# Degree counts of a graph network moved beside the normalising of layer 1, uneven transfers split at 112 partitions, and a preparation shared over three engines

## The chip, the cores and the metric

The kernel runs on one core of a Trainium2 chip. The metric is the device time of one launch in microseconds; the number that stands for a kernel is the median of its runs.

A core has a matrix engine (TensorE, PE in the profile), a vector engine (VectorE, DVE), a scalar engine (ScalarE, ACT), a general engine (GpSimd, POOL) and a queue that only issues transfers (SyncE, SP). Each executes its own instructions in order. Transfers are issued from SP's, ScalarE's and GpSimd's queues.

## What is computed

A graph has 6250 nodes with 128 features and 106250 edges, sorted by destination: 50000 random pairs in both directions and a loop at every node. Four layers follow each other; after each, x becomes layernorm(x + layer(x)).

```python
# layer 0: sums of edge attributes, then an MLP with 512 hidden
agg = segment_sum(edge_attr_128, dst, 6250)
y0  = relu(concat([agg, x]) @ W1 + b1) @ W2 + b2
# layer 1 (GIN): neighbours' sum, MLP with 256 hidden, two batchnorms over nodes
h  = (1 + eps) * x + segment_sum(x[src], dst, 6250)
y1 = relu(bn(relu(bn(h @ W1 + b1)) @ W2 + b2) + x)
# layer 2: two convolutions with the neighbours' mean
conv(x) = (segment_sum(x[src], dst) / count(dst)) @ W_l + b + x @ W_r
y2 = conv2(relu(conv1(x)))
# layer 3 (GAT, 3 heads): softmax over each node's edges, weighted sums, projection
alpha = leaky_relu(a_src[src] + a_dst[dst] + a_edge)
y3 = layernorm(x + gat(x, alpha) @ lin_W + lin_b)   # with its own scale and shift
```

Layer 3 also gives each node a loop of its own, whose edge term is the mean of its edges' terms. For that mean, for the mean of layer 2 and for finding a node's first edge, the kernel needs the number of edges up to each node.

## The kernel before, in words

**Tiles.** Nodes are taken as 50 blocks of 125 (`PB`, `NB5`), in 13 chunks (`CHUNKS`) of four blocks, the last of two. Edges are taken as 833 tiles of 128 (`NT`); as rows they stand in 119 partitions of 896 (`RB`, L). Node features exist twice: node-major (`xn`, 125 partitions) and feature-major (`xt`, 128 partitions).

**Preparation** (L84 to L189). The destinations (`dsti`), the destinations shifted by one edge (`prvi`) and the sources (`srci`) are loaded as 119 rows, 118 or 117 of them in one transfer each, on SP's and ScalarE's queues (L100 to L106). VectorE casts them, TensorE transposes them to tiles (`dsta` and `ix["src"]`), a matmul spreads the first row (`bc`), and VectorE makes differences (`relg`, `relb`) and seven tests of the data (`bad`); `fives` and `far` (L177 to L183) belong to one test. Their outcome is `flag` (L189), which every engine reads to branch into the main path (`general`).

**Sums over neighbours** (`neighbours`, L752 on), once in layer 1 and twice in layer 2. Most of a sum is done as a dense product: the count of edges between nodes, as a bf16 matrix in memory, is streamed by SP in pieces (`piece`) and multiplied with the features split in two bf16 halves (`arena`), in L819 (`sums`). For the last nodes the rows of a table in memory are gathered one tile of 128 edges at a time on GpSimd (L774, `row`), 183 tiles in each convolution, and added up by matmuls with a one-hot (L323, `both`), four groups of three tiles at a time, into `by_node`.

**Layer 1.** After the sums (690 to 1072 us), the second part has two stretches. In the first (pool `l1p`, L904 to L922) each of 13 parts of 500 nodes takes a hidden product (`hidden`, L876), a ScalarE activation (L914), a second product (L918), a ScalarE copy (L919) and VectorE statistics (L858) that free the PSUM tile. Beside it run `loops` (scans along the edges, L1207 to L1211) and `counted` (L529 to L560). In the second (pool `l1x`, L924 to L947) the second batchnorm, relu, residual, transposes (`nodes`, `features`), layernorm and `split` are done chunk by chunk, and table1 is stored (L940).

**`counted`.** For each block GpSimd gathers the destinations of 128 edges that surround each node's place (L416, `nd`, 50 gathers on 125 partitions). VectorE compares and sums them: L543 to L545, ten steps of five blocks. From the result (`upto`) come the places of each node's first edge (`start_of`), the reciprocal of its count (`rcnt`), and its last edge (`lasti`, L559).

**Layer 2** (1251 to 2187 us). `last_sums` (L637 to L642) gathers, for each block, the running sum at the node's last edge (`st`, 50 gathers by `lasti` on GpSimd). Table2 is stored from ScalarE's queue (L999). The second convolution stores x3 (L1049) and scatters the destination terms into `edst` (L1046, on GpSimd).

**Layer 3** (2187 to 3575 us). `edst` is loaded as `ed` (L1076; 119 rows), spread along the edges by scans (`along`, L1196 and L1211), and then 208 batches of edges are weighed and summed; their rows come by GpSimd gathers (L1065).

**What sets the order.** The source is written with generators that are pulled at chosen places (`next(degrees)`). A scheduler then orders the instructions of each engine by its own estimate of times, and inserts semaphore waits; tiles from a pool are reused when their readers are done. So an instruction's place in its engine's queue is fixed when the program is built.

Of the kernel before, what the change touches and what calls it, by code (L numbers as in the profile page):

```python
# [8 lines left out]
F32 = mybir.dt.float32  # L9
I32 = mybir.dt.int32  # L10
AF = mybir.ActivationFunctionType
OP = mybir.AluOpType
AX = mybir.AxisListType
# [6 lines left out]
F = 128  # L20
# [18 lines left out]
RT, RB = 7, 119  # L39
# [16 lines left out]
def gnn_kernel(ctx: ExitStack, tc: tile.TileContext, a: dict, out: bass.AP):  # L56
# [27 lines left out]
    with tc.tile_pool(name="ix", bufs=1) as sp, \  # L84
# [12 lines left out]
        def row(x):  # L97
            return x.rearrange("(p t) -> p t", p=1)

        nc.sync.dma_start(dsti[0:RB - 1, :], d[0:full].rearrange("(p t) -> p t", t=L))  # L100
        nc.sync.dma_start(dsti[RB - 1:RB, 0:E - full], row(d[full:E]))
        nc.scalar.dma_start(prvi[1:RB - 1, :], d[L - 1:full - 1].rearrange("(p t) -> p t", t=L))
        nc.scalar.dma_start(prvi[0:1, 1:L], row(d[0:L - 1]))
        nc.scalar.dma_start(prvi[RB - 1:RB, 0:E - full + 1], row(d[full - 1:E]))
        nc.sync.dma_start(srci[0:RB - 1, :], s[0:full].rearrange("(p t) -> p t", t=L))
        nc.sync.dma_start(srci[RB - 1:RB, 0:E - full], row(s[full:E]))  # L106
        dstf = sp.tile([RB, L], F32, name="dstf")
        nc.vector.tensor_copy(dstf, dsti)
        srcf = sp.tile([RB, L], F32, name="srcf")
        nc.vector.tensor_copy(srcf, srci)  # L110
        for k in range(RT):
            nc.gpsimd.tensor_copy(ix["df"][:, k:k + 1], dstf[:, k * 128:k * 128 + 1])

# [6 lines left out]
        nc.vector.tensor_reduce(bad[:RB, 0:1], vi, AX.X, OP.max)  # L120

        dsta = sp.tile([128, NT], F32, name="dsta")
        for x, to in ((dstf, dsta), (srcf, ix["src"])):
            by_row = to.rearrange("p (r k) -> p k r", k=RT)
            for k0 in range(0, RT, 4):
                kn = min(4, RT - k0)
                p = pp.tile([128, 4, 128], F32, name="xa_p")
                for k in range(k0, k0 + kn):
                    nc.tensor.transpose(p[:, k - k0, :RB], x[:, k * 128:(k + 1) * 128], ident[:RB, :RB])
                nc.vector.tensor_copy(by_row[:, k0:k0 + kn, :], p[:, :kn, :RB])  # L130

        sel = sp.tile([128, 128], F32, name="sel")
        nc.vector.memset(sel, 0.0)
# [2 lines left out]
        for c in range(0, NT, 417):  # L136
            w = min(417, NT - c)
            p = pp.tile([128, 512], F32, name="bc_p")
            nc.tensor.matmul(p[:, :w], lhsT=sel, rhs=dsta[:, c:c + w], start=True, stop=True)
            nc.vector.tensor_copy(bc[:, c:c + w], p[:, :w])  # L140
        relg, relb = ix["relg"], ix["relb"]
        by_g = dsta[:, 0:NG * GT].rearrange("p (g j) -> p g j", j=GT)
        bcg = bc[:, 0:NG * GT].rearrange("p (g j) -> p g j", j=GT)
# [31 lines left out]
        nc.vector.tensor_scalar(bad[:, 6:7], bcg[:, 4 * Q0, 0:1], float(ND), None, op0=OP.is_ge)  # L175

        fives = sp.tile([128, NT], F32, name="fives")  # L177
        nc.vector.tensor_scalar(fives, dsta, -(GD // 2), 1.0 / GD, op0=OP.add, op1=OP.mult)
        nc.vector.tensor_scalar(fives, fives, ROUND, None, op0=OP.add)
        nc.vector.tensor_scalar(fives, fives, -ROUND, None, op0=OP.add)  # L180
        far = sp.tile([128, NT], F32, name="far")
        nc.vector.tensor_tensor(far[:, 0:830], fives[:, 1:831], fives[:, 0:830], op=OP.subtract)
        nc.vector.tensor_reduce(top[:, 0:1], far[:, 0:830], AX.X, OP.min)  # L183
        nc.vector.tensor_scalar(bad[:, 3:4], top[:, 0:1], 1.0, None, op0=OP.is_lt)
        p = pp.tile([128, 512], F32, name="bc_p")
# [1 line left out]
        nbad = sp.tile([1, 1], F32, name="nbad")  # L187
        nc.vector.tensor_reduce(nbad, p[0:1, 0:7], AX.X, OP.add)
        nc.vector.tensor_scalar(flag, nbad, 0.0, None, op0=OP.is_equal)  # L189

    ordered = nc.values_load(flag[0:1, 0:1], min_val=0, max_val=1, skip_runtime_bounds_check_because=FLAG)
    with tc.If(ordered) as cond:
# [10 lines left out]
def by_windows(ctx: ExitStack, tc: tile.TileContext, a: dict, out: bass.AP, consts, ix):  # L203
# [52 lines left out]

    def by_block(table, blocks):
        return table[blocks[0] * PB:(blocks[-1] + 1) * PB, :].rearrange("(b p) f -> p b f", p=PB)

    def over(x, n):  # L260

        return x.rearrange("p (b f) -> p b f", f=1).to_broadcast([PB, x.shape[1], n])
# [266 lines left out]
    def counted(pool):  # L529


        thn = pool.tile([128, NB5], F32, name="node_col")
        nc.gpsimd.iota(thn, pattern=[[PB, NB5]], base=1, channel_multiplier=1,
                       allow_small_or_imprecise_dtypes=True)
        nc.vector.memset(upto[:, 0:1], 0.0)
        nd = pool.tile([128, NB5, 128], I32, name="nd")
        edges_from(a["dst"], n0i[:PB], nd[:PB])
        for c in range(NB5 // M):
            yield
            cs = slice(c * M, (c + 1) * M)  # L540
            up = upto[:PB, 1 + cs.start:1 + cs.stop]
            lt = pool.tile([128, M, 128], F32, name="ndlt")
            nc.vector.tensor_tensor(lt[:PB], nd[:PB, cs], over(thn[:PB, cs], 128), op=OP.is_lt)  # L543
            nc.vector.tensor_reduce(up, lt[:PB], AX.X, OP.add)
            nc.vector.tensor_add(up, up, n0[:PB, cs])  # L545

        shift = pool.tile([PB, 2, PB], F32, name="shifts")
        nxt = pool.tile([128, 2], F32, name="nexts")
        for i, by in enumerate((1.0, float(1 - PB))):
            nc.vector.tensor_scalar(nxt[:, i:i + 1], part, by, None, op0=OP.add)  # L550
            nc.vector.tensor_scalar(shift[:, i, :], iota[:PB, :PB], nxt[:PB, i:i + 1], None, op0=OP.is_equal)
        p = (yield).tile([128, 4, F], F32, name="node_p")[:, 0, :]
        start = p[:PB, 0:NB5]
        nc.tensor.matmul(start, lhsT=shift[:, 0, :], rhs=upto[:PB, 1:], start=True, stop=False)
        nc.tensor.matmul(start, lhsT=shift[:, 1, :], rhs=upto[:PB, 0:NB5], start=False, stop=True)
        nc.vector.tensor_copy(start_of[:PB], start)
        nc.vector.tensor_tensor(rcnt[:PB], upto[:PB, 1:], start, op=OP.subtract)
        nc.vector.reciprocal(rcnt[:PB], rcnt[:PB])
        nc.vector.tensor_scalar(lasti[:PB], upto[:PB, 1:], -1.0, None, op0=OP.add)  # L559
        yield  # L560
# [149 lines left out]
    with tc.tile_pool(name="l0w", bufs=2) as work, \  # L710
# [5 lines left out]
        for blocks in CHUNKS:  # L716
            b0, nb = blocks[0], len(blocks)
            w = nb * PB
            cs = slice(b0 * PB, b0 * PB + w)
            xk = work.tile([128, 4, F], F32, name="xk")  # L720
            xk = xk[:PB, :nb, :]
            nc.sync.dma_start(xk, by_block(a["x"], blocks))
            xc = work.tile([128, 4 * PB], F32, name="xc")
            features(xc[:, :w], xk, tp)
            ht = work.tile([128, 4, 4 * PB], F32, name="ht")
            for m in range(4):
                hp = hps.tile([128, 4 * PB], F32, name="hp")
                ms = slice(m * 128, (m + 1) * 128)
                nc.tensor.matmul(hp[:, :w], lhsT=w1[:, 0, ms], rhs=acc0[:, cs], start=True, stop=False)
                nc.tensor.matmul(hp[:, :w], lhsT=w1[:, 1, ms], rhs=xc[:, :w], start=False, stop=True)  # L730
                nc.scalar.activation(ht[:, m, :w], hp[:, :w], AF.Relu, bias=b1[:, m:m + 1])
            if last is not None:
                last()
            yp = yps.tile([128, 4, F], F32, name="yp")
            for j in range(nb):
                for m in range(4):
                    nc.tensor.matmul(yp[:PB, j, :], lhsT=ht[:, m, j * PB:(j + 1) * PB], rhs=w2[:, m, :],  # L737
                                     start=(m == 0), stop=(m == 3))
            y = work.tile([128, 4, F], F32, name="y")
            y = y[:PB, :nb, :]  # L740
            nc.vector.tensor_tensor(y, yp[:PB, :nb, :], row_over(b2[:PB], nb), op=OP.add)
            nc.vector.tensor_add(y, y, xk)
            layernorm(xn[:PB, b0:b0 + nb, :], y)
            nc.sync.dma_start(by_block(tables[0], blocks), xn[:PB, b0:b0 + nb, :])
            split(xn[:PB, b0:b0 + nb, :], blocks, work)

            def last(b0=b0, nb=nb, cs=cs):
                features(xt[:, cs], xn[:PB, b0:b0 + nb, :], tp)
# [93 lines left out]
    with tc.tile_pool(name="l1", bufs=1) as wp:  # L842
# [81 lines left out]
        with tc.tile_pool(name="l1x", bufs=2) as work, tc.tile_pool(name="zps", bufs=3, space=bass.MemoryType.PSUM) as zps, \  # L924
                tc.tile_pool(name="tps", bufs=2, space=bass.MemoryType.PSUM) as tp:
            last = None
            for blocks in CHUNKS:
# [6 lines left out]
                z = nodes(h0[:, cs], nb, zps)  # L934
                if last is not None:
                    last()
                if b0 < 40:
                    next(degrees)
                layernorm(xn[:PB, b0:b0 + nb, :], z)
                nc.sync.dma_start(by_block(tables[1], blocks), xn[:PB, b0:b0 + nb, :])  # L940
                split(xn[:PB, b0:b0 + nb, :], blocks, work)

                def last(b0=b0, nb=nb, cs=cs):
# [7 lines left out]
    with tc.tile_pool(name="l2", bufs=1) as wp, tc.tile_pool(name="l2w", bufs=2) as work, \  # L951
# [22 lines left out]
        def take(k, p):  # L974
# [3 lines left out]
            def late():  # L978
# [11 lines left out]
                for j in range(0, len(blocks), 2):  # L990
# [5 lines left out]
                                             start=(m_ == 0), stop=(m_ == 1))  # L996
                    nc.scalar.copy(pn[:PB, b0 + j:b0 + j + 2, :], yp[:PB, :, 0, :])
                    nc.vector.tensor_tensor(x[:, j:j + 2, :], x[:, j:j + 2, :], yp[:PB, :, 1, :], op=OP.add)
                nc.scalar.dma_start(by_block(tables[2], blocks), pn[:PB, b0:b0 + len(blocks), :])  # L999
            return late  # L1000

        ends = last_sums()
# [5 lines left out]
    with tc.tile_pool(name="l2bw", bufs=2) as work, \  # L1008
# [8 lines left out]
        def then(k):  # L1017
# [27 lines left out]
            for j in range(nb):  # L1045
                nc.gpsimd.indirect_dma_start(  # L1046
                    out=edst, out_offset=bass.IndirectOffsetOnAxis(ap=start_of[:PB, b0 + j:b0 + j + 1], axis=0),
                    in_=ad[:PB, j, :], in_offset=None)
            nc.scalar.dma_start(by_block(x3, blocks), xw[:PB, :nb, :])  # L1049

        neighbours(None, take, then, tables[2], len(matrix) - 2)
    outer.close()
# [20 lines left out]
    with tc.tile_pool(name="fill", bufs=1) as fp, \  # L1073
            tc.tile_pool(name="fps", bufs=2, space=bass.MemoryType.PSUM) as pp:
        ed = fp.tile([RB, L, 4], F32, name="ed")
        nc.sync.dma_start(ed.rearrange("p t f -> p (t f)"), edst.rearrange("(p t) f -> p (t f)", t=L))  # L1076
        filled = fp.tile([RB, L, H], F32, name="filled")
        along(tc, consts, ix["first"], [ed[:, :, h] for h in range(H)], [filled[:, :, h] for h in range(H)], fp, pp)()
        nc.vector.tensor_add(filled, filled, aeb)
# [796 lines left out]
```

## Time and profile before

| what | value |
|---|---|
| time, median of three runs | 3329.91 us (3328.71 to 3332.3) |
| time of the profiled execution | 3577.21 us |
| its span in the trace | 3575.3 us |
| mean granted clock of TensorE | 0.82 |
| busy: PE, DVE, POOL, ACT | 2624.6, 1837.7, 1671.1, 910.8 us |
| flag ready | 36.3 us |
| sums of layer 1 end | 1072 us |
| layer 1's first stretch, second stretch | to 1173, to 1239 us |
| first sums of layer 2 | 1251 us |
| `ed` loaded | 2207.9 to 2225.4 us |

The profiled execution is 7.4% longer than the median of the others; its durations are read as shares of its own span. In the profile a group line gives the line in the code, the engine, the operation, the written and read tiles with shapes, the number of instructions, then their busy time in us and the mean of one in ns, then the idle time of that engine just before them and what ended it. A timeline line begins with its start and its length in us; the bracket holds the idle time before it and what ended that. A step of the chain is start, length, what.

### The profile page before, as it was taken

To read this page: it belongs to the slowest core of one execution; us is meant where nothing else is said; L and a number is where in the kernel's file an instruction comes from. 1 tells how busy PE (TensorE), PEld (TensorE's weight loads), DVE (VectorE), ACT (ScalarE), POOL (GpSimd) and SP (SyncE) were. 2 spreads that over 40 slices of the span, in tenths; PEclk is the share of its full clock that TensorE was granted. 3 is DMA by queue.
4 is the path that set the end of the run, shared out by engine and by line. 5 is a ranking of instruction groups with operands and counts; after the bars stand their busy time and mean duration, and the time that the engine had idled before them with its cause. 6 is when DMAs were issued, how large, how long until landed. Compare 5 with 4: busy or idle time off the path is not lost.

```text
span 3575.3 us, 43560 instructions
## 1 busy us (share of the span) xinstructions
PE 2624.6 (73%) x14544; PEld 1618.5 (45%) x14544; DVE 1837.7 (51%) x6113; ACT 910.8 (25%) x1657; POOL 1671.1 (47%) x1684
## 2 busy tenths in 40 slices
PE   2788879899995599999787893666565666666565
PEld 1334335544442344445343342555554555555554
DVE  4899994478214800000211122666565666666666
ACT  0587874300002400002100010222222222222222
POOL 3000002277607755430556424666666666666662
PEclk9677779999997599999898896777777777777777
DMA  5588871387751356563665553222222222222221
GB/s 155 167 278 279 274 248 48 105 245 228 220 164 51 82 181 205 182 183 96 184 179 153 169 166 90 52 58 58 54 61 58 56 57 58 55 60 59 57 58 33
DMA packets 333524, 461.85 MB, mean 129 GB/s; under 512 B 43998, under 2 KB 217854, under 8 KB 332933
## 3 DMA queue, kind: packets, MB, share of 16 engines
q1 hardware_dynamic: 250754, 278.98, 26.2%
q0 software_dynamic: 54912, 105.86, 12.4%
q10 hardware_dynamic: 27624, 74.14, 5.6%
q8 instruction: 117, 1.92, 0.2%
q14 instruction: 117, 0.96, 0.1%
HBM read 375.30 MB, written 83.36 MB: 128 GB/s over the span
## 4 chain that ended last, share of the span: by engine, by line
PE 52%; DVE 22%; issue 12%; DMA 4%; POOL 3%; another core or an unknown queue 3%; ACT 2%; DVEq 1%; SPq 0%; ACTq 0%; POOLq 0%
PE sums L819 25%; PE o L1162 10%; DVE okey L616 5%; DVE olow L614 4%; PE w_p L1141 4%; POOL nd L416 2%; DVE w L1151 2%; PE both L323 2%; DVE w L1136 1%; PE yp L995 1%; ACT w L1153 1%; PE yp L737 1%; PE fp L1102 1%; DVE mx L1144 1%
## 5 line engine op out<-in xcount | busy, mean ns | idle before, releaser
L1065 POOL DMA_INDIRECT rows<-x,srca x831 | 841.5, 1013 | 490.3 <-issue 213.4
L819 PE MATMUL sums<-piece,arena 125*128 125x500 bf16 x4500 | 1021.1, 383 | 51.1 <-issue 40.0
L819 PEld LDWEIGHTS <-arena 125*128 125x128 bf16 x4500 | 435.6, 98 | 591.4 <-issue 122.4
L774 POOL DMA_INDIRECT row<-table,srca x549 | 542.1, 987 | 335.7 <-issue 142.5
L1162 PE MATMUL o<-rows,w 128*120 128x132 f32 x2078 | 440.1, 364 | 245.1 <-issue 132.2
L1162 PEld LDWEIGHTS o<-rows,w 128*120 128x120 f32 x2078 | 378.1, 255 | 290.1 <-issue 159.7
L619 ACT CAST arena<-made 128x1000 bf16<-128x1000 f32 (+1 forms) x260 | 313.5, 1262 | 63.9 <-PE made L617 55.9
L1153 ACT ACTIVATE w<-w 128x720 f32<-128x720 f32 x208 | 167.0, 803 | 521.6 <-DVE w L1151 368.5
L617 PE MATMUL made<-okey,olow 128*128 128x250 bf16 x1000 | 248.4, 330 | 62.4 <-ACT arena L619 28.4
L616 DVE TENSOR_SCALAR okey<-iok,key 128x250 bf16<-128x250 bf16 x1000 | 289.6, 290 | 0.0
L1141 PE MATMUL w_p<-ident,w 128*120 128x128 f32 x1248 | 230.7, 328 | 65.1 <-DVE w L1136 39.1
L1144 DVE TENSOR_REDUCE mx<-w_p 120x1 f32<-120x768 f32 x208 | 198.0, 952 | 151.7 <-PE o L1162 82.6
L1151 DVE TENSOR_TENSOR w<-w,both 128x720 f32<-128x720 f32 x208 | 187.1, 900 | 162.0 <-remote 89.1
L614 DVE TENSOR_SCALAR olow<-iob,low 128x128 bf16<-128x128 bf16 x1000 | 254.7, 255 | 0.0
L1141 PEld LDWEIGHTS w_p<-ident,w 128*120 128x120 f32 x1248 | 187.2, 169 | 80.3 <-issue 49.6
L325 ACT COPY by_node<-both 128x128 f32<-128x128 f32 (+1 forms) x48 | 12.7, 265 | 756.6 <-PE both L323 479.8
L334 DVE TENSOR_TENSOR onehot<-iota,relg 128x384 f32<-128x384 f32 x118 | 64.2, 547 | 272.7 <-PE both L323 140.9
L617 PEld LDWEIGHTS <-olow 128*128 128x128 bf16 x1000 | 108.0, 113 | 184.9 <-DVE okey L616 89.6
L1136 DVE TENSOR_TENSOR w<-oh,z 128x720 f32<-128x720 f32 x208 | 186.7, 898 | 0.2 <-DVE acc L1169 0.2
L690 POOL MEMSET ea<- 128x128 f32 x1 | 0.5, 465 | 397.9 <-PE sums L323 397.9
L1168 PE MATMUL both<-ident,on 120*128 120x120 f32 x208 | 70.3, 338 | 108.2 <-DVE w L1151 95.2
L1148 PE MATMUL both<-ident,mx 120*128 120x120 f32 x208 | 73.0, 351 | 91.2 <-DVE acc L1169 69.6
(283 smaller groups left out, 3188.5 us busy)
## 6 DMA issues: line engine op xcount, KB each, us to landing
piece<-edges SPq DMA_DIRECT2D x300, 625.0 KB
edges<-arena ACTq DMA_DIRECT2D x100, 625.0 KB
ea<-in_edge_attr_dram SPq DMA_DIRECT2D x69, 768.0 KB
loop<-x SPq DMA_DIRECT2D x208, 68.0 KB
rows<-x,srca POOLq DMA_INDIRECT x831
row<-table,srca POOLq DMA_INDIRECT x549
eat<-in_edge_attr_dram POOLq DMA_DIRECT2D x28, 236.0 KB
table<-xn SPq DMA_DIRECT2D x24, 250.0 KB
```

Of the source, the lines that this page charges most:

```text
L614: nc.vector.tensor_scalar(o, iob, low[:, g:g + 1], None, op0=OP.is_equal)
L616: nc.vector.tensor_scalar(w, iok, key[:, g:g + 1], None, op0=OP.is_equal)
L617: nc.tensor.matmul(p[:, i, 0:NB5 * GD], lhsT=o, rhs=w, start=True, stop=True)
L619: nc.scalar.copy(to, p[:, 0:n, 0:NB5 * GD].rearrange("p i (h d) -> p i h d", d=GD))
L774: nc.gpsimd.indirect_dma_start(out=r[:, j, :], out_offset=None, in_=table, in_offset=bass.IndirectOffsetOnAxis(ap=ix["src"][:, t:t + 1], a ...
L819: nc.tensor.matmul(p, lhsT=xp[:PB, h, i, :], rhs=t[:PB, :, (h - h0) * SC:(h - h0 + 1) * SC], start=(h == 0 and i == 0), stop=(h == NB5 - 1 ...
L1065: nc.gpsimd.indirect_dma_start(out=r[:, j, :], out_offset=None, in_=x3, in_offset=bass.IndirectOffsetOnAxis(ap=ix["src"][:, BT * b + j:BT ...
L1136: nc.vector.tensor_tensor(w, oh.to_broadcast([128, S, H, BW]), z.rearrange("p j (h w) -> p j h w", w=1).to_broadcast([128, S, H, BW]), op= ...
L1141: nc.tensor.transpose(tp[:, j // 3, j % 3 * 128:(j % 3 + 1) * 128], w[:, j, :, :].rearrange("p h w -> p (h w)"), ident)
L1144: nc.vector.tensor_reduce(mx, tp[:, :, 0:384], AX.XY, OP.max)
L1151: nc.vector.tensor_tensor(wf, wf, mb.rearrange("p (j h) w -> p j (h w)", j=1) .to_broadcast([128, S, H * BW]), op=OP.subtract)
L1162: nc.tensor.matmul(o, lhsT=wf[:, j, :], rhs=rr, start=(j == 0), stop=(j == S - 1))
```

## The change

There are three edits.

**1. The comparisons of `counted`.** They are taken per chunk (twelve times four blocks, once two) instead of ten times five blocks, and are pulled in the second stretch, each before its chunk's layernorm; their scratch tile is `rest` of that stretch's pool. In the built program the comparison of the first chunk stands on VectorE in the first stretch, behind the scans, and the other twelve in the second; `start_of`, `rcnt` and `lasti` come at the end of the second stretch. GpSimd's queue then reads: 5 gathers of `st`, 24 of `row`, 26 of `st`, 12 of `row`, 19 of `st`, 147 of `row`; before it read 50 of `st` and 183 of `row`.

```diff
     def counted(pool):
...
-        for c in range(NB5 // M):
-            yield
-            cs = slice(c * M, (c + 1) * M)
+        for blocks in CHUNKS:
+            work = yield
+            cs, nb = slice(blocks[0], blocks[-1] + 1), len(blocks)
             up = upto[:PB, 1 + cs.start:1 + cs.stop]
-            lt = pool.tile([128, M, 128], F32, name="ndlt")
-            nc.vector.tensor_tensor(lt[:PB], nd[:PB, cs], over(thn[:PB, cs], 128), op=OP.is_lt)
-            nc.vector.tensor_reduce(up, lt[:PB], AX.X, OP.add)
+            lt = work.tile([128, 4, F], F32, name="rest")
+            nc.vector.tensor_tensor(lt[:PB, :nb], nd[:PB, cs], over(thn[:PB, cs], 128), op=OP.is_lt)
+            nc.vector.tensor_reduce(up, lt[:PB, :nb], AX.X, OP.add)
             nc.vector.tensor_add(up, up, n0[:PB, cs])
...
-                if b0 < 40:
-                    next(degrees)
+                degrees.send(work)
                 layernorm(xn[:PB, b0:b0 + nb, :], z)
```

**2. Transfers in two parts.** The loads of `dsti`, `prvi` and `srci` become 112 partitions and the rest (6, 5, 6). A helper stores 112 and 13 partitions in place of 125, for tables 0 and 1 (SP's queue), table2 and x3 (ScalarE's): 52 stores more. `ed` is loaded as 112 partitions on SP's queue and 7 on ScalarE's.

```diff
+    def keep_nodes(queue, table, blocks, x):
+
+        to = by_block(table, blocks)
+        for p0, p1 in ((0, 112), (112, PB)):
+            queue.dma_start(to[p0:p1], x[p0:p1, :len(blocks), :])
...
-        nc.sync.dma_start(dsti[0:RB - 1, :], d[0:full].rearrange("(p t) -> p t", t=L))
+        for p0, p1 in ((0, 112), (112, RB - 1)):
+            nc.sync.dma_start(dsti[p0:p1, :], d[p0 * L:p1 * L].rearrange("(p t) -> p t", t=L))
...
-            nc.scalar.dma_start(by_block(x3, blocks), xw[:PB, :nb, :])
+            keep_nodes(nc.scalar, x3, blocks, xw)
...
-        nc.sync.dma_start(ed.rearrange("p t f -> p (t f)"), edst.rearrange("(p t) f -> p (t f)", t=L))
+        for p0, p1, queue in ((0, 112, nc.sync), (112, RB, nc.scalar)):
+            queue.dma_start(ed[p0:p1].rearrange("p t f -> p (t f)"),
+                            edst[p0 * L:p1 * L, :].rearrange("(p t) f -> p (t f)", t=L))
```

In the built program the last of the four last scatters into `edst` stands two row gathers earlier in GpSimd's queue than before.

**3. Preparation.** The copies of `dsta` and `bc` out of PSUM are ScalarE's, `fives` and `far` are GpSimd's, and the cast, transposes and copies of the sources (still VectorE's) stand last in the source.

```diff
-        srcf = sp.tile([RB, L], F32, name="srcf")
-        nc.vector.tensor_copy(srcf, srci)
...
-        for x, to in ((dstf, dsta), (srcf, ix["src"])):
+
+        def tiles_of(x, to, copy):
...
-                nc.vector.tensor_copy(by_row[:, k0:k0 + kn, :], p[:, :kn, :RB])
+                copy(by_row[:, k0:k0 + kn, :], p[:, :kn, :RB])
+
+        tiles_of(dstf, dsta, nc.scalar.copy)
...
-            nc.vector.tensor_copy(bc[:, c:c + w], p[:, :w])
+            nc.scalar.copy(bc[:, c:c + w], p[:, :w])
...
-        nc.vector.tensor_scalar(fives, dsta, -(GD // 2), 1.0 / GD, op0=OP.add, op1=OP.mult)
-        nc.vector.tensor_scalar(fives, fives, ROUND, None, op0=OP.add)
-        nc.vector.tensor_scalar(fives, fives, -ROUND, None, op0=OP.add)
+        nc.gpsimd.tensor_scalar(fives, dsta, -(GD // 2), 1.0 / GD, op0=OP.add, op1=OP.mult)
+        nc.gpsimd.tensor_scalar(fives, fives, ROUND, None, op0=OP.add)
+        nc.gpsimd.tensor_scalar(fives, fives, -ROUND, None, op0=OP.add)
...
-        nc.vector.tensor_tensor(far[:, 0:830], fives[:, 1:831], fives[:, 0:830], op=OP.subtract)
+        nc.gpsimd.tensor_tensor(far[:, 0:830], fives[:, 1:831], fives[:, 0:830], op=OP.subtract)
...
+        srcf = sp.tile([RB, L], F32, name="srcf")
+        nc.vector.tensor_copy(srcf, srci)
+        tiles_of(srcf, ix["src"], nc.vector.tensor_copy)
```

More of the change, by code (lines that the diff above doesn't have):

```diff
@@ L98, in row @@
             return x.rearrange("(p t) -> p t", p=1)
-        nc.sync.dma_start(dsti[0:RB - 1, :], d[0:full].rearrange("(p t) -> p t", t=L))
+        for p0, p1 in ((0, 112), (112, RB - 1)):
+            nc.sync.dma_start(dsti[p0:p1, :], d[p0 * L:p1 * L].rearrange("(p t) -> p t", t=L))
         nc.sync.dma_start(dsti[RB - 1:RB, 0:E - full], row(d[full:E]))
-        nc.scalar.dma_start(prvi[1:RB - 1, :], d[L - 1:full - 1].rearrange("(p t) -> p t", t=L))
+        for p0, p1 in ((1, 113), (113, RB - 1)):
+            nc.scalar.dma_start(prvi[p0:p1, :], d[p0 * L - 1:p1 * L - 1].rearrange("(p t) -> p t", t=L))
         nc.scalar.dma_start(prvi[0:1, 1:L], row(d[0:L - 1]))
         nc.scalar.dma_start(prvi[RB - 1:RB, 0:E - full + 1], row(d[full - 1:E]))
-        nc.sync.dma_start(srci[0:RB - 1, :], s[0:full].rearrange("(p t) -> p t", t=L))
+        for p0, p1 in ((0, 112), (112, RB - 1)):
+            nc.sync.dma_start(srci[p0:p1, :], s[p0 * L:p1 * L].rearrange("(p t) -> p t", t=L))
         nc.sync.dma_start(srci[RB - 1:RB, 0:E - full], row(s[full:E]))
@@ L743, in by_windows @@
             layernorm(xn[:PB, b0:b0 + nb, :], y)
-            nc.sync.dma_start(by_block(tables[0], blocks), xn[:PB, b0:b0 + nb, :])
+            keep_nodes(nc.sync, tables[0], blocks, xn[:, b0:b0 + nb, :])
             split(xn[:PB, b0:b0 + nb, :], blocks, work)
@@ L936, in by_windows @@
                     last()
-                if b0 < 40:
-                    next(degrees)
+                degrees.send(work)
                 layernorm(xn[:PB, b0:b0 + nb, :], z)
-                nc.sync.dma_start(by_block(tables[1], blocks), xn[:PB, b0:b0 + nb, :])
+                keep_nodes(nc.sync, tables[1], blocks, xn[:, b0:b0 + nb, :])
                 split(xn[:PB, b0:b0 + nb, :], blocks, work)
@@ L998, in late @@
                     nc.vector.tensor_tensor(x[:, j:j + 2, :], x[:, j:j + 2, :], yp[:PB, :, 1, :], op=OP.add)
-                nc.scalar.dma_start(by_block(tables[2], blocks), pn[:PB, b0:b0 + len(blocks), :])
+                keep_nodes(nc.scalar, tables[2], blocks, pn[:, b0:b0 + len(blocks), :])
             return late
```

## The prediction, made before the changed kernel ran

> **What bounds the kernel now.** I read the chain of waits first, to learn which stages end on which engine; then the busy time of each engine in the two stretches that the comparisons leave and enter; then the groups of instructions there; then single lines of the timeline at the start, and where layers 2 and 3 begin.
>
> The chain by engine is mostly TensorE and VectorE, and it names four transfers that the diff touches. Columns of the last two lines: start in us, length in us, what.
>
> ```profile
> PE 52%; DVE 22%; issue 12%; DMA 4%; POOL 3%; another core or an unknown queue 3%; ACT 2%; DVEq 1%; SPq 0%; ACTq 0%; POOLq 0%
> ...
> 3.06 19.52 DMA srci<-in_src_dram
> ...
> 2207.91 17.48 DMA ed<-edst
> ```
>
> The second part of layer 1 has two stretches: hidden layers (about 1084 to 1173 us), then normalising (1176 to 1235). The windows give busy us of each engine (and instruction counts):
>
> ```profile
> core 0: us, PE busy (x) PEld busy (x) DVE busy (x) ACT busy (x) POOL busy (x), PEclk, DMA share, GB/s
> 1084.00:1172.80 88.80, 49.32 (x100) 21.29 (x100) 30.96 (x63) 25.69 (x39) 66.71 (x54) 0.77 0.18 47
> 1176.50:1235.00 58.50, 29.58 (x97) 19.30 (x97) 57.00 (x202) 29.15 (x58) 48.44 (x34) 0.53 0.26 50
> ```
>
> In the first no compute engine is full; in the second VectorE is busy 57.0 of 58.5 us. The groups of the first stretch say what sets its pace:
>
> ```profile
> L416 POOL DMA_INDIRECT nd<-in_dst_dram,n0i x43 | 54.4, 1265 | 13.1 <-issue 13.1
> ...
> L876 PE MATMUL hp<-xn,l1w 128*128 128x500 f32 x42 | 23.3, 664 | 25.6 <-DVE cin L1209 25.6
> ...
> L544 DVE TENSOR_REDUCE upto<-ndlt 125x5 f32<-125x640 f32 x10 | 8.1, 811 | 0.1
> L543 DVE TENSOR_TENSOR ndlt<-nd,node_col 125x640 f32<-125x640 int32 x9 | 7.4, 825 | 47.0 <-DMA nd<-in_dst_dram,n0i 47.0
> ```
>
> VectorE stands idle 47.0 us for nd: a comparison needs five more gathers, GpSimd issues one every 1.265 + 0.30 = about 1.5 us, and behind the waiting comparison stand the statistics (L858) that free TensorE's PSUM. That is the stretch's bound: 50 x 1.5 = 75 us of gathers for 44 us of matmuls.
>
> [...] from 15 to 23 us, with only srci loading, the DMA share is 0.11, two of 16. [...]
>
> **The change part by part.** The sums are made against the profiled execution (3577.2 us, span 3575.3); it is 7.4% longer than the median, 3329.9, and I carry differences over unscaled.
>
> *A, preparation.* The flag (L189) ends at 36.3 and everything waits for it.
>
> ```profile
> 14.54 0.63 DVE L108 CAST dstf<-dsti 119x896 f32<-119x896 int32 x1 [11.24 <-DMA dsti<-in_dst_dram]
> ...
> 26.02 1.01 DVE L144 TENSOR_TENSOR relg<-dsta,bc 128x831 f32<-128x831 f32 x1
> ...
> 36.20 0.14 DVE L189 TENSOR_SCALAR flag<-nbad 1x1 int32<-1x1 f32 x1
> ```
>
> dsti [...] lands at about 7.0 (prvi[...] moves at 276 GB/s or more, dsti and srci at 55): 7.5 gained. From the cast to relg are 11.5 us now, with srci's wait and cast, its copies and a third of fives on VectorE in between; with the four copies on ScalarE I count 7.2 (cast 0.6, transposes 1.3, copies of 0.6 to 1.0 each, table load 1.3 beside the load): 4.3 gained. From relg to the flag are 10.3: fives' two rest steps and far (0.58 + 0.60 + 1.02) leave, srcf's cast and copies (0.6 + 1.5) come; 9.7. fives and far on GpSimd, after its copies and memsets (1.82, 0.27, 2.78): [...] needed at about 14. [...] Sum -7.5 - 4.3 - 0.6 + 1.0 = -11.4 (-8 to -13.5).
>
> *B1, comparisons leave the first stretch.* What remains is TensorE: 13 chunks of 8 passes at 0.42 us = 3.36, 43.7 from 1084, so it ends near 1127.5 instead of 1172.9: -45.4 (-35 to -49). One comparison stays there in the built program, after the scans (L1211, three of about 2.05 us): its gathers have landed.
>
> *B2, they enter the second.* VectorE is full there, so all counts: a compare and a reduce of 125x512 at 0.60 net each (they read 0.82 at 640, ends overlapping; the residual L360 of 512 reads 0.68) and the add 0.09: 1.29 x 11 + 0.75 = +15 (12 to 18). Behind each on VectorE wait the layernorm and the transposes fed by it. Gathers are no wait: chunk c needs gather 4c+3, landed at 1080 + 6c, run at 1132 + 6.2c.
>
> *B3, lasti comes at the end of the second stretch.* Now it is ready at 1157.7 and all 50 gathers of st run under the second stretch:
>
> ```profile
> 1158.00 1.20 POOL L639 DMA_INDIRECT st<-esum,lasti  x1 [1.93 <-DVE lasti L559]
> ...
> 1245.11 1.18 POOL L774 DMA_INDIRECT row<-table,srca  x1 [3.52 <-DMA piece<-edges]
> ...
> 1347.86 0.86 PE L323 MATMUL both<-row,onehot 128*32 128x128 f32 x24
> ```
>
> Built, GpSimd's queue reads st x5, row x24, st x26, row x12, st x19, then rows. With E the end of the last normalising (1238.7 now): st at 1.5 us and rows at 1.25 put the first rows at E+9.0 instead of E+6.4 (+2.8 to TensorE's start), the 24th at E+39, st to E+78, twelve rows to E+93 (2.2 to land: E+95.4, needed at E+91.9), st to E+122, twelve rows to E+137, landed E+138.9. TensorE needs those at 1347.86 = E+109.1. So it loses 29.8 in all (20 to 43: it gets there sooner if the 14 us that it idles on "issue" before 1284 are the profiler's). Then rows take 15 us per group of 20 to 24 on TensorE: GpSimd catches up, one stall. B together: -45.4 + 15 + 29.8 = -0.6.
>
> *C, table stores.* Table2's last store ends on five engines, and the next gather waits 8.35 us behind it and the pieces ("1710.61 L774 row, from piece<-edges"). [...] -3.5 (-1 to -4). Tables 0 and 1: a piece ends last or st is in front: 0. 52 stores more, at 0.3 us of issue: SP's 39 rows lie in queues that wait for data; ScalarE's 26, 8 us over 480 us in which it is a quarter busy at most, hide under sums (L819). If not, +8.
>
> *D, edst and ed.* The last scatter moves past two gathers (2 x 1.25 = -2.5) and its predecessor lands in 2.6 rather than 4.6 beside a shorter x3 store (-1.5; 0 to -2). ed, 17.48 us [...], moves in about 9 [...], the remaining 7 partitions on ScalarE's queue beside it: -8.5 (-4 to -11). VectorE's first scan of layer 3 waits for it 38.66 us: all counts. D: -12.5.
>
> Sum: -11.4 - 0.6 - 3.5 - 12.5 = -28; 3577.2 becomes 3549, and 3329.9 becomes 3302.
>
> **Rivals.**
> - *R1, the gathers' order costs nothing*: TensorE has other work at the third and fourth group, or the gathers are cheaper without the profiler. For: it does idle before them now. Against: q3's rows stand behind 50 st in one queue. Then -28 - 30 = 3272.
> - *R2, slower: the first stretch doesn't shorten.* Its 25.6 us of TensorE idle are put to the scans' carry (cin, L1209), which may keep TensorE's queue on VectorE after the comparisons are gone. B2 and B3 stay. With B1 at nothing: 3302 + 45 = 3347. It decides from a B1 under 17 us, that is a stretch of over 72 us (5.5 a chunk). Against: the chunks at its end, free of nd, run at 3 us each.
> - *R3, a worse stall*: 43 for 30, 3315.
> - *R4, the change doesn't do what it says*: rows of 112 move no faster as something else bounds them; A keeps 7.5, C 3.5, ed 8.5 and 1.5 go: 3302 + 21 = 3323. Against: the 0.11.
>
> **How the numbers follow.** Forecast 0.60 (3285 to 3312), R1 0.11, R2 0.09, R3 0.13, R4 0.07. The range 3278 to 3324 leaves out most of R1 and R2. A measurement of this kernel tells about 0.2%, 6.7 us, from no change: faster is under 3323, which the forecast, R1, R3 and half of R4 give, 0.86; the other half of R4 is no change, with R2's near end 0.06; slower 0.08.
>
> **What would show it.** The flag near 25; the first stretch at 44 to 55 us with no VectorE wait for nd; the second at 73, VectorE full; GpSimd's first st after it; TensorE waiting some 30 us for row before its fourth group of `both`; ed in 9. Wrong it would be if TensorE's carry wait stays, if GpSimd's four operations end after 14 us, or if no stall shows in layer 2.

## The result and the profile after

The changed kernel takes 3317.0 us (median of 7 runs, 3311.7 to 3321.8), the kernel before 3333.2 beside it; the ratio is 0.9946, interval 0.9934 to 0.9958. That is 16 us less, against 28 forecast.

The profiled execution of the changed kernel took 3321.8 us (span 3320.0). The first profile of the kernel before, at 3577 us, holds waits of TensorE that its runs near 3330 us don't have, so differences below are taken from a second profile of before (span 3329.1, run e1) unless the first is named, and ratios from runs side by side.

The two stretches of layer 1's second part in the changed kernel, busy us of each engine, in the same view as in the prediction:

```profile
core 0: us, PE busy (x) PEld busy (x) DVE busy (x) ACT busy (x) POOL busy (x), PEclk, DMA share, GB/s
1067.00:1110.00 43.00, 41.75 (x103) 18.77 (x102) 18.23 (x44) 26.25 (x40) 34.51 (x28) 1.00 0.24 71
1113.00:1186.00 73.00, 30.11 (x98) 19.90 (x98) 72.62 (x241) 31.29 (x61) 20.53 (x16) 0.50 0.21 55
```

The first is now TensorE's, 41.75 of 43.0 us busy, at a granted clock of 1.00 for 0.77; the second is VectorE's as before, and longer. The groups of the first stretch show that nothing waits for `nd` any more. The matmul of `hp` has lost its idle time, and a pass takes 0.58 where it took 0.66 to 0.70 us:

```profile
L429 POOL DMA_INDIRECT nd<-in_dst_dram,n0i x28 | 35.7, 1274 | 8.5 <-issue 8.5
L931 PE MATMUL hp<-h,l1w 128*128 128x500 f32 x48 | 23.5, 588 | 0.3 <-ACT h L927 0.2
L889 PE MATMUL hp<-xn,l1w 128*128 128x500 f32 x45 | 21.6, 582 | 0.0
...
L556 DVE TENSOR_TENSOR rest<-nd,node_col 125x512 f32<-125x512 int32 x1 | 0.7, 693 | 0.1
```

The preparation on VectorE's timeline (start, length, what, and in brackets the idle time before it), from the cast of the destinations to the flag:

```profile
5.94 0.63 DVE L111 CAST dstf<-dsti 119x896 f32<-119x896 int32 x1 [2.63 <-DMA dsti<-in_dst_dram]
...
10.05 1.09 DVE L116 TENSOR_TENSOR firstb<-dstf,prvi 119x896 f32<-119x896 f32 x1 [3.02 <-DMA prvi<-in_dst_dram]
11.18 1.65 DVE L120 SCALAR_TENSOR_TENSOR vi<-firstb 119x896 f32<-119x896 f32 x1
...
13.87 1.01 DVE L148 TENSOR_TENSOR relg<-dsta,bc 128x831 f32<-128x831 f32 x1
...
18.39 1.47 DVE L163 CAST basei<-late 1x61 int32<-1x61 f32 x1
...
22.44 1.02 DVE L187 TENSOR_REDUCE top<-far 128x1 f32<-128x830 f32 x1
...
25.33 0.15 DVE L193 TENSOR_SCALAR flag<-nbad 1x1 int32<-1x1 f32 x1
```

The flag is ready at 25.5 instead of 36.2 us. At the other end, the chain of waits has the load of `ed` at half its length (17.48 before):

```profile
2126.86 2.57 DMA edst<-ad,start_of
2129.51 9.39 DMA ed<-edst
```

What was gained there and in the first stretch is largely spent at the start of layer 2. First GpSimd's queue, where `st` comes between and ahead of rows (5 of `st` from 1189.5, 24 of `row` from 1197.3, 26 of `st` from 1228.2, 12 of `row` from 1267.1, 19 of `st` from 1282.1 us, the built order); then TensorE, which meets the third and fourth group of `both` without their rows:

```profile
1197.27 1.30 POOL L787 DMA_INDIRECT row<-table,srca  x1 [0.31 <-issue]
...
1228.16 1.20 POOL L652 DMA_INDIRECT st<-esum,lasti  x1 [0.30 <-issue]
...
1267.08 0.96 POOL L787 DMA_INDIRECT row<-table,srca  x1 [0.30 <-DMA st<-esum,lasti]
...
1282.10 1.20 POOL L652 DMA_INDIRECT st<-esum,lasti  x1 [0.30 <-issue]
```

```profile
1249.15 0.86 PE L336 MATMUL both<-row,onehot 128*32 128x128 f32 x24
...
1277.56 0.63 PE L336 MATMUL both<-row,onehot 128*32 128x128 f32 x2 [2.91 <-DMA row<-table,srca]
...
1313.27 0.61 PE L336 MATMUL both<-row,onehot 128*32 128x128 f32 x2 [8.33 <-DMA row<-table,srca]
1316.79 0.64 PE L336 MATMUL both<-row,onehot 128*32 128x128 f32 x2 [2.91 <-DMA row<-table,srca]
...
1326.86 0.64 PE L336 MATMUL both<-row,onehot 128*32 128x128 f32 x2 [0.58 <-DMA row<-table,srca]
1327.43 5.53 PE L832 MATMUL sums<-piece,arena 125*128 125x500 bf16 x15
```

A group of 24 matmuls that takes 0.86 us when its rows are there takes 14 us (from 1313.27), after 8.33 of waiting. In the whole trace TensorE waits 46.3 us for rows before `both`, in e1 17.9.

### The profile page after: what moved, and what is told of

It reads as the page before. It is cut to its first block, busy times and chain, and to the rows that moved or that the text cites. A ratio compares the mean times of both kernels' runs of the same rounds, so it can differ in the third digit from the quotient of the medians.

```text
span 3320.0 us, 43665 instructions
## 1 busy us (share of the span) xinstructions
PE 2498.5 (75%) x14544; PEld 1537.7 (46%) x14544; DVE 1834.3 (55%) x6114; ACT 913.5 (28%) x1661; POOL 1678.8 (51%) x1688
## 4 chain that ended last, share of the span: by engine, by line
PE 32%; DVE 12%; DMA 7%; POOL 6%; issue 6%; ACT 3%; DVEq 1%; ACTq 0%; POOLq 0%; SPq 0%
PE sums L832 15%; PE o L1176 8%; DMA rows<-x,srca 4%; DVE w L1165 3%; POOL rows L1077 3%; ACT w L1167 3%; POOL row L787 2%; PE w_p L1155 2%; PE yp L1007 1%; DVE w L1150 1%; DVE mx L1158 1%; DMA row<-table,srca 1%; PE fp L1116 1%; PE both L336 1%; POOL st L652 1%
## 5 line engine op out<-in xcount | busy, mean ns | idle before, releaser
L832 PE MATMUL sums<-piece,arena 125*128 125x500 bf16 x4500 | 1001.0, 379 | 10.1 <-DMA piece<-edges 10.1
L1077 POOL DMA_INDIRECT rows<-x,srca x831 | 852.0, 1025 | 303.9 <-issue 181.6
L1176 PE MATMUL o<-rows,w 128*120 128x132 f32 x2078 | 390.1, 334 | 283.4 <-ACT w L1167 283.4
L1176 PEld LDWEIGHTS o<-rows,w 128*120 128x120 f32 x2078 | 335.0, 229 | 324.5 <-ACT w L1167 324.4
L630 PE MATMUL made<-okey,olow 128*128 128x250 bf16 x1000 | 252.3, 332 | 60.0 <-ACT arena L632 25.5
L1155 PE MATMUL w_p<-ident,w 128*120 128x128 f32 x1248 | 214.2, 312 | 47.0 <-DVE w L1150 44.3
L1155 PEld LDWEIGHTS w_p<-ident,w 128*120 128x120 f32 x1248 | 173.9, 160 | 60.2 <-issue 38.5
L1165 DVE TENSOR_TENSOR w<-w,both 128x720 f32<-128x720 f32 x208 | 186.9, 899 | 23.3 <-PE both L1162 17.9
L1135 DVE TENSOR_TENSOR z<-rows,zed 128x12 f32<-128x12 f32 x208 | 34.6, 166 | 200.1 <-DMA rows<-x,srca 199.1
L343 DVE TENSOR_TENSOR arena<-arena,both 128x32 f32 x183 | 34.1, 186 | 176.8 <-PE both L340 164.1
```

The lines of the kernel that those rows point to most:

```text
L630: nc.tensor.matmul(p[:, i, 0:NB5 * GD], lhsT=o, rhs=w, start=True, stop=True)
L832: nc.tensor.matmul(p, lhsT=xp[:PB, h, i, :], rhs=t[:PB, :, (h - h0) * SC:(h - h0 + 1) * SC], start=(h == 0 and i == 0), stop=(h == NB5 - 1 ...
L1077: nc.gpsimd.indirect_dma_start(out=r[:, j, :], out_offset=None, in_=x3, in_offset=bass.IndirectOffsetOnAxis(ap=ix["src"][:, BT * b + j:BT ...
L1155: nc.tensor.transpose(tp[:, j // 3, j % 3 * 128:(j % 3 + 1) * 128], w[:, j, :, :].rearrange("p h w -> p (h w)"), ident)
L1165: nc.vector.tensor_tensor(wf, wf, mb.rearrange("p (j h) w -> p j (h w)", j=1) .to_broadcast([128, S, H * BW]), op=OP.subtract)
L1176: nc.tensor.matmul(o, lhsT=wf[:, j, :], rhs=rr, start=(j == 0), stop=(j == S - 1))
```

## The experiments

My theory before them: each part gives about what its place in the trace shows, and the moved comparisons cost in layer 2 what they save in layer 1, because `lasti` comes late and all 50 gathers of `st` enter GpSimd's queue among the rows. The rivals: the queue's order costs nothing (then the transfers or the preparation have to explain the shortfall), or the splits are hidden.

**e1: the kernel before again, for its profile.** No edit.

> The kernel before, unchanged, for a second profile, because the first one ran 7.4% longer than the median while that of the changed kernel did not. If the first profile was a disturbed execution, layer 3 takes near 1190 us here (2139 to 3320 in the changed kernel; 1350 in the first profile) and the waits on issue of TensorE in layer 2 are gone; if the code of the kernel before is slow there under any profile, layer 3 takes 1350 again. The time without a profile stays at 3325 to 3340 either way.

Span 3329.1 us, time 3330.9. Layer 3, from the first scan of `ed` to the end, takes 1175 us, not 1350, and no matmul of `sums` (L819) waits on issue. The first stretch takes 92.5 us here (1073.95 to 1166.40), the last normalising ends at 1232.3. These lines give the time at which TensorE is due to read the rows of the fourth group when nothing stalls it (the last line):

```profile
1242.95 0.64 PE L323 MATMUL both<-row,onehot 128*32 128x128 f32 x2 [4.97 <-DMA row<-table,srca]
1243.52 21.49 PE L819 MATMUL sums<-piece,arena 125*128 125x500 bf16 x90
1264.94 0.86 PE L323 MATMUL both<-row,onehot 128*32 128x128 f32 x22
...
1328.77 0.86 PE L323 MATMUL both<-row,onehot 128*32 128x128 f32 x24
```

That is E+96.5, with E the end of the last normalising; the prediction read E+109.1 from the first profile. There the same 90 matmuls of `sums` take 32.6 us instead of 21.4, of which 7.2 are waits on issue:

```profile
1251.44 17.18 PE L819 MATMUL sums<-piece,arena 125*128 125x500 bf16 x70
1270.13 0.37 PE L819 MATMUL sums<-piece,arena 125*128 125x500 bf16 x1 [1.51 <-issue]
...
1284.03 0.86 PE L323 MATMUL both<-row,onehot 128*32 128x128 f32 x22
```

**e2: the comparisons alone.** The kernel before with

```diff
-        for c in range(NB5 // M):
-            yield
+        for blocks in CHUNKS:
+            work = yield
...
-                if b0 < 40:
-                    next(degrees)
+                degrees.send(work)
```

> Only the comparisons move (edit 1); transfers and preparation stay as before. My theory: the first stretch shrinks by some 48 us, the second grows by 12, the first sums of layer 2 start 7 us later after it, and the third and fourth group of gathered rows cost 10 and 21: sum +2, so 3328 to 3340 for a before of 3333. Rival, the gathers' order costs nothing without a profile: -30 to -36, near 3300. Rival, a worse stall: +10 or more.

Ratio 1.0039 (1.0026 to 1.0052): 13 us slower (9 to 17). Against e1, from the first batchnorm's statistics on: first stretch 45.0 for 92.5 (-47.4); second 78.0 for 65.9 (+12.1); from E to the first sums 15.5 for 11.2 (+4.3); from there to the end of the fourth group 124.0 for 86.1 (+37.9); and the 15 sums after the wait take 5.64 for 3.34 (+2.3). Sum +9, at the low end of the interval. The stall is 4.3 + 37.9 + 2.3 = 44.5, where I had expected 7 + 10 + 21 = 38 and a sum of +2; the rival of a worse stall is what happened. Its lines, from the first sums to the last wait of the fourth group:

```profile
1209.59 20.33 PE L819 MATMUL sums<-piece,arena 125*128 125x500 bf16 x90
...
1333.01 0.64 PE L323 MATMUL both<-row,onehot 128*32 128x128 f32 x2 [0.60 <-DMA row<-table,srca]
```

So the moved comparisons by themselves made the kernel slower, and the gain came from the other parts.

**e3: stores and `ed` alone.** The kernel before with

```diff
-                nc.scalar.dma_start(by_block(tables[2], blocks), pn[:PB, b0:b0 + len(blocks), :])
+                keep_nodes(nc.scalar, tables[2], blocks, pn[:, b0:b0 + len(blocks), :])
...
+        for p0, p1, queue in ((0, 112, nc.sync), (112, RB, nc.scalar)):
```

and the same for tables 0 and 1 and x3.

> Only the stores of the tables and of x3 and the load of ed are split (edit 2 without the loads of the preparation). My theory: the start of layer 3 gains 12 (ed 8, scatter 4) and the start of layer 2's second convolution 2 to 4: -14, near 3319. Rival, hidden anyway or the 52 more issues cost what they gain: within 4 of before.

Ratio 0.995 (0.9937 to 0.9963): -17 us (-21 to -12). In its trace the last VectorE step of layer 2 and the first scan of layer 3 lie 26.3 apart for 39.4 in e1 (-13.1), and the end of the first convolution's last product and the end of the first group of rows 24.9 for 28.4 (-3.5). The two sum to -16.6, so the time shows no cost of the 52 extra issues.

**e4: the preparation alone**, its three loads split too.

```diff
+        for p0, p1 in ((0, 112), (112, RB - 1)):
+            nc.sync.dma_start(dsti[p0:p1, :], d[p0 * L:p1 * L].rearrange("(p t) -> p t", t=L))
...
+        tiles_of(dstf, dsta, nc.scalar.copy)
...
+        nc.gpsimd.tensor_scalar(fives, dsta, -(GD // 2), 1.0 / GD, op0=OP.add, op1=OP.mult)
```

> Only the preparation is changed, its loads of dsti, prvi and srci as 112 partitions and the rest included (edit 3 and the first part of edit 2). My theory: the flag comes 10.9 us earlier and all that follows with it: -9 to -14, near 3322. Rival, the first loads of layer 0 or its planner take it back: within 4 of before.

Ratio 0.9976 (0.9966 to 0.9987): -8 us (-11 to -4), for -9 to -14 expected; its flag is ready at 24.9 for 36.2, 11.3 sooner. The three parts sum to 13 - 17 - 8 = -12 with an uncertainty of about 7, in agreement with -18 (-22 to -14) from the ratio of the whole.

**e5: `st` tied to the means.** The changed kernel, in which each chunk's indices are made from its mean of layer 2, times zero, so that its four gathers cannot come sooner.

```diff
+            nc.vector.scalar_tensor_tensor(lf[:PB, :len(bs)], m[:PB, 0:len(bs)], 0.0,
+                                           upto[:PB, 1 + bs[0]:2 + bs[-1]], op0=OP.mult, op1=OP.add)
+            nc.vector.tensor_scalar(lasti[:PB, bs[0]:bs[-1] + 1], lf[:PB, :len(bs)], -1.0, None, op0=OP.add)
+            for _ in bs:
+                next(ends)
...
-        neighbours(before, take, None, tables[1], len(matrix), lambda i: next(ends, None))
+        neighbours(before, take, None, tables[1], len(matrix))
```

> The changed kernel, but each chunk's four gathers of st are tied by data to that chunk's mean in layer 2, so that GpSimd's queue has 36 gathers of row in front of the first st and the rest spread. Theory, the lost time of the moved comparisons is st standing ahead of row in GpSimd's queue: the third and fourth group of both wait for nothing, the first sums start 3 to 7 us sooner, and the time falls by 38 to 45 from 3317, to 3272 to 3280. Rival, GpSimd's gathers are the limit as such and the order is indifferent: within 7 of 3317, as the waits move to later groups.

This and all later runs fell on chips where the kernel before takes 3574 to 3581 us, so the absolute figures do not apply. Ratio to before 0.9866 (0.984 to 0.9892). In the trace no group waits for a row after the first two pairs, and the fourth group starts at E+113.3. What the changed kernel itself does on such a chip shows in e9. The groups of e5:

```profile
1234.32 0.85 PE L336 MATMUL both<-row,onehot 128*32 128x128 f32 x20
1254.32 0.86 PE L336 MATMUL both<-row,onehot 128*32 128x128 f32 x24
1278.14 0.86 PE L336 MATMUL both<-row,onehot 128*32 128x128 f32 x24
1301.94 0.94 PE L336 MATMUL both<-row,onehot 128*32 128x128 f32 x24 [1.30 <-issue]
```

**e6: and six comparisons in the first stretch.** As e5; six steps are tied to the statistics of every second part there.

```diff
+            if gate is not None:
+                nc.vector.scalar_tensor_tensor(thn[:PB, cs], gate[:PB, 0:nb], 0.0, thn[:PB, cs],
+                                               op0=OP.mult, op1=OP.add)
...
+                if k in (1, 3, 5, 7, 9, 11):
+                    degrees.send((work, s2[:, PARTS[k][0], :]))
```

> As the run before, and six of the comparisons tied by data to every second part of the first stretch, where VectorE has room. Theory, VectorE is full in the second stretch and TensorE alone sets the first: five comparisons more leave the second stretch at 1.0 to 1.3 us each, so 5 to 6 us below the run before; the first stretch stays at 45 us. Rival, the comparisons pace the first stretch again by their gathers: no gain or up to 10 us slower than the run before.

Ratio to before 0.9859 (0.9825 to 0.9893), not to be told from e5, so the 5 to 6 us expected are not shown in the time. The stretches are clearer: first 45.8 for 44.9, second 74.5 for 78.0, and from E to the first sums 10.8 for 15.1.

**e7: `ed` alone.** The kernel before with the `ed` hunk of e3 only.

> The kernel before with the load of ed alone as 112 partitions on SP's queue and 7 on ScalarE's. Theory: 17.5 us become 9.4 and all of it counts: -8, near 3320. Rival, something else in layer 3's start ends at that time: within 3 of before.

Ratio 0.9983 (0.9965 to 1.0002): -6 us, not clear of nothing. The last VectorE step of layer 2 and the first scan are 30.7 apart in its trace for 38.8 in the first profile of before: -8.1.

**e8: the first loads alone.** The kernel before with the first diff lines of e4, for the three tiles.

> The kernel before with the loads of dsti, prvi and srci alone split at 112. Theory: dsti's cast starts 8.5 us sooner, the sources are no longer waited for, and the flag comes 8 to 9 us sooner with VectorE and TensorE as the limit behind it; the time falls by 6 to 9. Rival, the order of the engines is the limit and the loads give less than 4.

Ratio 0.9971 (0.9953 to 0.9989): -10 us (-17 to -4). The flag is ready at 28.7, 7.6 sooner than in the first profile of before.

**e9, e10, e11: the changed kernel, e5 and e6 side by side on one chip.** No new edits.

> The changed kernel, unchanged, on the same chip as the two runs beside it, since the runs before came from a chip on which the kernel before takes 3581 and not 3328. Ratio to before: 0.9946 where before takes near 3330. Where before takes near 3580, its waits on issue in layer 2 already delay the groups of both by 13, so that the stall of the gathers is 30 and not 44, and the ratio lies near 0.991.

> The changed kernel with st tied to the means of layer 2, again, beside the changed kernel. Theory, the stall is the order in GpSimd's queue: 35 to 45 below the changed kernel where before takes near 3330, 25 to 32 where it takes near 3580. Rival, the order is indifferent: within 5 of the changed kernel.

> The same with six comparisons tied to the first stretch, again. Theory: 3 to 6 below the run with st tied alone, since the second stretch read 74.5 for 78.0 us in its first profile and the first stretch 45.8 for 44.9. Rival, the gathers of nd pace the first stretch: no gain.

Ratios to before (3574.3): changed kernel 1.0006 (0.9985 to 1.0027), e10 0.9893 (0.9858 to 0.9927), e11 0.9868 (0.983 to 0.9906). Tying `st` gives 42 us over the changed kernel beside it (3577.9 to 3535.4), more than the 25 to 32 expected: the order of the queue costs that much on this chip. My expectation for e9, a ratio near 0.991 and a stall of only 30, was wrong: on this chip the change gains nothing. From E to the end of the fourth group e9 takes 166.3 us for 110.0 in the first profile of before, a loss of 56. TensorE starts that group at 1355.3, 165 after E (e10: 113.5), and on the way there its lines show mostly waits that the profile calls issue, in place of waits for rows, which are 10.6 us in the whole trace. The waits of TensorE in e9, in us, with number and longest:

```profile
PE o L1176 <- issue: 119.1, 72, 4.2
...
PE sums L832 <- issue: 49.6, 59, 2.2
```

e1 has no such lines. So on this chip the order of the queue is shown to cost time, but not by way of the waits for rows that e2 and the changed kernel show where before takes near 3330 us. The version with `st` tied was not run on a chip of that kind; what it gains there is not shown.

e11 against e10 is 8 us, more than the 3 to 6 expected, and unclear by itself. From layer 1's statistics to layer 2's first sums the traces take 131.1 us for 138.0, in e6 against e5 and again in e11 against e10.

**e12: the last version once more.**

> The version with st tied to the means and six comparisons tied to the first stretch once more, for its ratio to the kernel before on whichever chip it falls: 0.979 to 0.984 where before takes near 3330 (0.9946 less 40 to 50 us of 3330), 0.983 to 0.989 where it takes near 3580, as in the two runs so far. Rival, the gain was of those two runs only: over 0.99.

Ratio 0.9853 (0.9834 to 0.9873), 52 us below before (3579.6 to 3527.8), as expected. It is the same kernel as e6 and e11, and on the chip of e9 faster than both the kernel before and the changed one. Its ratio on a chip of the other kind was not measured.

## Why the prediction was right, and where its steps were off

The range held (3278 to 3324 for 3317), the sign too; the size was 28 for 16. The forecast's own 3285 to 3312 did not hold: what came is rival R3, at 3315. There is luck in it: the due times were read from a profile of 3577 us, and on a chip where the kernel before takes 3574 us the change gains nothing (e9).

- **A, preparation, -11.4: near.** The flag came 10.7 sooner (36.2 to 25.5), the time fell by 8 (4 to 11) in e4. Against e1 the cast came 8.3 sooner (at 5.9, not 7.0), the way from the cast to `relg` was 3.7 shorter (4.3 forecast), and from `relg` to the flag it was 1.3 longer (0.4 forecast, though the terms given there sum to 10.2 and not to 9.7). The loads' share of 7.5 agrees with e8's flag (7.6).
  - Behind the cast `prvi` was a new wait of 3.0 us (L116) that I had not priced.
  - Four VectorE steps took 3.2 us longer than before, beside GpSimd's (`vi` 1.65 for 1.07, L153 1.20 for 0.53, `late` 0.85 for 0.18, L163 1.47 for 0.17), where the forecast's +1.0 was my estimate; L153 and L163 held up what stands behind them by 2.0 us, `late` by nothing. But `relg` (L148) and the step behind it (L151) took 1.01 us as before, with GpSimd's `fives` steps beside them too. What slows the four is not shown.
  - GpSimd's four operations ended at 19.8, 13.9 after the cast, just inside the 14 that was named as a sign of being wrong. They took 9.0 us and were hidden, as I had estimated, since VectorE needed them at 22.4.
- **B1, -45.4: right.** e2 shows -47.4. R2 (the first stretch doesn't shorten) falls: the carry's wait is gone with the comparisons.
- **B2, +15: right in kind**, 12.1 in e2. A comparison's three steps cost about 1.0 us each chunk and not 1.29, worked out as 12.1 over 12 chunks.
- **B3, +29.8: the term that was too small.** The queue's arithmetic held: by the prediction the last rows land at E+138.9, and the last wait of e2's fourth group ends at 1333.0, which is E+138.9. What failed is "TensorE needs those at 1347.86 = E+109.1". That due time was taken from a profile in which the `sums` before the first group take 32.6 us; where they take 21.4, it is E+96.5. The stall was 44.5. The prediction named this doubt and gave it to R3 (43, so 3315), and R3's mechanism was the forecast's own. The 14 us of issue that it named are 7.2 in the lines; the rest of the difference is matmuls that took longer.
- **C, -3.5 and D, -12.5: right.** e3 shows 3.5 and 13.1 in the trace and 17 (12 to 21) in time. (Of the 52 extra stores 26 are SP's, not 39.) `ed` went from 17.5 to 9.4, 8.1 for 8.5, with a DMA share of 0.91 (2129.5 to 2138.9 us) for 0.56 (2208 to 2225 in the first profile), row gathers beside it in both. The first loads on SP's queue moved at a share of 0.13 in the first profile (6.1 to 14.2) and of 0.98 in the changed kernel's (3.2 to 4.2); a store of four blocks into table2 at 0.32, about five of 16 engines (1700.0 to 1701.9), and at 0.94 (1661.4 to 1662.3). R4 falls for `ed` and `dsti`. That 112 partitions would move faster was my estimate; why their share is higher is not shown. But not every split transfer came sooner: `prvi` had moved by about 6 us before, where the traffic falls to 50 GB/s, and L116 now waits for it until 10.05; the DMA share from 6 to 8 us is 0.82 for 0.12.
- **R1 falls** with e2, which is slower though only the comparisons move, and with e10, where the order alone is worth 42 us on the other kind of chip.

With what the traces show, -10.7 for A, -47.4 and +12.1 and +44.5 for B, -3.5 for C and -13.1 for D, the sum becomes -18, the value that the ratio gives.

## What to carry to other kernels

When an engine's result is moved later, list every transfer whose indices hang on it, and lay them into the queue that issues them: here 50 gathers that had cost nothing under other work came to stand ahead of the rows that TensorE was due to read. This program's scheduler didn't keep them back; a data dependence did (e5, e10). And take a due time from a profile that agrees with the runs' own time: one that is 7% longer may hold stalls that the runs don't have.

## What was not expected of the hardware

- The same kernel took 3325 to 3342 us on some chips and 3558 to 3601 on others. On the slower ones TensorE shows issue waits, 37 to 50 us in `sums` and 119 to 146 in L1162 (its lines in other versions); in the first profile of before, which has them too, layer 3 runs at a granted clock of 0.72 to 0.73 instead of 0.80 to 0.81 in the changed kernel's. In e9's layer 2, up to the fourth group, most of them fall between 1225 and 1308 us, in a long run of GpSimd gathers with hardly a pause; beside a run of twelve, from 1336 to 1351, there are none. What makes them is open. A change that makes GpSimd's gathers denser beside TensorE gained 16 us on one kind of chip and nothing on the other; that the gathers are the link was not tested.
- On GpSimd the first `fives` step, from `dsta` into `fives` with two operations, took 1.30 us; the two in place, with one operation each, took three, and the two-input step 1.57:

```profile
10.59 1.30 POOL L182 TENSOR_SCALAR fives<-dsta 128x833 f32<-128x833 f32 x1
11.98 3.04 POOL L183 TENSOR_SCALAR fives<-fives 128x833 f32<-128x833 f32 x1
15.10 3.07 POOL L184 TENSOR_SCALAR fives<-fives 128x833 f32<-128x833 f32 x1
18.25 1.57 POOL L186 TENSOR_TENSOR far<-fives 128x830 f32<-128x830 f32 x1
```

e4 has the same four within 0.3 us. Whether writing in place or VectorE beside them makes the three was not tried.
